# A graph network in one kernel: every engine keeps the emitted order, the timetable is told of three more buffers and gets new numbers

## The chip, the cores and the metric

The kernel runs on one core of one Trainium2 chip. The metric is the device time of one execution in microseconds (us); of several executions the median counts. Five engines matter here: TensorE (PE, matrix products, with weight loads shown as PEld), VectorE (DVE), ScalarE (ACT), GpSimd (POOL, hardly used) and SyncE (SP), which only issues transfers. Each has its own instruction queue, and the queues meet by semaphores.

## The reference

Sixteen graphs of 1024 nodes with 128 features each, a 0/1 adjacency with about 16 neighbours to a node, and four layers; each adds its output to `x` and normalises the rows.

```python
x = _layernorm(x + _L0_gnn_ref(x, adj, U))          # relu((mask^T x) U / deg)
x = _layernorm(x + _L1_gnn_ref(x, adj, Wv, ...))    # masked softmax attention, q, k, v with relu
x = _layernorm(x + _L2_gnn_ref(x, adj, W, a))       # GAT, 4 heads: leaky relu, softmax, sum
x = _layernorm(x + _L3_gnn_ref(x, adj, nodemask, ...))  # 3 x SAGE on a dilated adjacency, then linear
```

The last layer first dilates the adjacency. Row by row, a node with more than ten neighbours drops those whose running number is a multiple of half its count, and the column entry goes too:

```python
num = jnp.sum(nbi)
sf = jnp.where(num > T_DIL, (num + K_DIL - 1) // K_DIL, 1)
rank = jnp.cumsum(nbi)
rm = row & (rank % sf == 0)
carry = carry.at[n].set(row & keep)
carry = carry.at[:, n].set(carry[:, n] & keep)
```

## The kernel before

Two stages follow one another. `fuse` does layers 0 to 2 for 16 graphs (a batch below is one graph) and beside them the dilation. It leaves the features `x3` and the dilated adjacency `adt_d` in DRAM. `sage` does the last layer from there. This case changes only `fuse`.

A graph's adjacency is eight tiles of 128 rows by 1024. All work of `fuse` is written as ten generators, which run at the same time:

- `loads` and `signs`: adjacency tiles come in through SP, DVE makes the 0/1 pattern `has` (L332), ACT the complement `over` (L336).
- `dilate`: for the batch ahead. Eight scans on DVE (L354) give `ranked`, a running count along each row; PE turns blocks and DVE matches them (`turn`, `match`, L368, L378); two rounds and a last one decide what is dropped (ACT distances L426, DVE L441, PE counts L452); `lost` corrects (L495, ACT L519, DVE L528, which writes the dropped entries over `ranked`); `stays` makes the new pattern on PE (L541 to L547), and `store` evacuates it on ACT (L557) and sends it out through SP (L559).
- `layer0`: features (`py`) and the gather (L656).
- `layer1`, `scores`, `values`: keys, the attention scores (L744) with their minimum (L752) and exponential (L755), then transposes and the product with the values (L779).
- `layer2`, `sides`, `layer2_sums`: `weights` makes `st`, then the chain `top` (L882), `peak`, `peaks` (L887), `ps_cap` (L890), `cap` (L896), `ac` (L899), `src` (L917) and `pieces` (L924 to L933); `sides` makes sign tiles `sg` on ACT (L818) and masks them into `g` on DVE (L827); the sums use `pieces` against `has` (L968) and against `g` (L998).

Each generator yields a `Step` ahead of the instructions it is going to emit: an engine, a price in us, marks that must have been set, and places in rings of buffers that it takes or gives back. `Loom.run` is a planner in Python, run when the program is built. It keeps a clock for each engine. Of all heads it looks for the one that can start first, and among the steps of that engine which can start within a small window after it, it takes the one that is due first. Then the generator emits these instructions. A step's due time is the batch number times a period plus the phase of its part, with the prices of the steps before it in that part stretched by a factor:

```python
self.due = b * period + phase
self.due += self.step.cost * self.stretch
```

So the order in which the kernel emits is a whole timetable across engines. It knows the prices, a handoff time of 0.3 us between engines (0.5 us ahead of PE), and the rings it is told of: PSUM buffers (`two`, `one`, `dps`), `g`, `pr`, `a`, `w2k`, `over`. It didn't know that scans need `ranked` back, which has a single buffer (`p1`), that `sg` has two (`p2`), or that `adt` has two. The emitted order is then given to the compiler of the framework, which holds a dependency graph and a scheduler of its own: emitted order is a priority there, and each engine's queue can come out in another order.

All transfers named above are on SP's queue[...].

Of the kernel before, what the change touches and what calls it, by code (L numbers as in the profile page):

```python
# [7 lines left out]
F32 = mybir.dt.float32  # L8
# [6 lines left out]
F8 = mybir.dt.float8e4  # L15
# [5 lines left out]
P = 128  # L21
# [159 lines left out]
def fuse(S, ctx, a, x3, adt_d, viol, B=16):  # L181
# [20 lines left out]
    tc, nc = S.tc, S.nc  # L202
# [5 lines left out]
    N, TWOS, NEVER, ROUNDS, OVER = 8 * P, 2.0**24, 1e5, 2, 10  # L208
# [138 lines left out]
    def dilation(k, c):  # L347
# [2 lines left out]

        ranked[c] = p1.tile([P, 8, N], BF16, name="ranked")
        for r in range(8):
            yield Step("DVE", 2.2, after=(f"has {k} {r}",))
            V.tensor_tensor_scan(  # L354
                ranked[c][:, r, :], has[c][:, r, :], links[c][:, r, EDGE - 1 : EDGE - 1 + N].bitcast(U8),
                0.0, ALU.add, ALU.subtract,
            )
# [72 lines left out]
        for i in range(ROUNDS):  # L430
# [26 lines left out]
            sums = []  # L457
# [93 lines left out]

        def store(i, ps_n):
            r, f = i // 2, i % 2 * 512
            yield Step("ACT", 0.48, after=(f"stays {k} {i}",), give=[("dps", 0)])
            if f == 0:
                rows.append(p2.tile([P, N], F8, name="adt"))
            nc.scalar.activation(rows[-1][:, f : f + 512], ps_n, AF.Relu, scale=1.0 / LINK, saturate=False)  # L557
            if f:
                nc.sync.dma_start(adt_d[c, r], rows[-1])  # L559

        rows = []
# [4 lines left out]
    class Norm:  # L566


        def __init__(self, y):
            self.y = y  # L570
            self.st = sm.tile([P, 8, 6], F32, name="ln_st")

        def take(self, c):
            V.bn_stats(self.st[:, c, :], self.y[:, c, :])
# [1 line left out]
        def apply(self, mark):  # L576

            yield Step("DVE", 1.9)
            t = sm.tile([P, 6, 8, 1], F32, name="ln_t")
            both, apart, var, y, z, nb = (t[:, i, :, :] for i in range(6))  # L580
            e, o, se, so = (self.st[:, :, i : i + 1] for i in (1, 4, 2, 5))
            V.tensor_tensor(apart, e, o, ALU.subtract)
            V.tensor_tensor(var, se, so, ALU.add)
            V.scalar_tensor_tensor(apart, apart, P / 4.0, apart, ALU.mult, ALU.mult)
            V.tensor_tensor(var, var, apart, ALU.add)
            V.tensor_scalar(var, var, 1.0 / P, 1e-5, ALU.mult, ALU.add)

            V.tensor_scalar(y.bitcast(I32), var.bitcast(I32), -0.5, GUESS, ALU.mult, ALU.add)
            for _ in range(3):
                V.tensor_tensor(z, y, y, ALU.mult)  # L590
                V.scalar_tensor_tensor(z, z, -0.5, var, ALU.mult, ALU.mult)
                V.scalar_tensor_tensor(y, z, 1.5, y, ALU.add, ALU.mult)
            V.tensor_tensor(both, e, o, ALU.add)
            V.scalar_tensor_tensor(nb, both, -0.5, y, ALU.mult, ALU.mult)
            rs = y
            for q in range(2):
                yield Step("ACT", 1.55, mark=f"{mark} {q}")
                for c in range(4 * q, 4 * q + 4):
                    nc.scalar.activation(
                        self.y[:, c, :], self.y[:, c, :], AF.Identity, bias=nb[:, c, :], scale=rs[:, c, :]  # L600
                    )
# [156 lines left out]
    def values():  # L758
        for b in each:
            yield b, "values"  # L760
            yield Step(None, 0.0, after=(f"x1 {b} 1",))
            x2 = x01[b]
            norm = Norm(x2)
            for ib in range(8):
                yield Step("PE", 0.87, after=(f"pr {b} {ib}",), take=[("two", "p")], give=[("pr", ib)])
                pr, tot = made.pop((b, ib))
                ps_f = two.tile([P, 8, P], F32, name="ps_flip", tag="two")
                for q in range(2):
                    flip4(ps_f[:, 4 * q : 4 * q + 4, :], lambda c: pr[:, c * P : (c + 1) * P], q)
                yield Step("ACT", 0.89, give=[("two", "p")])  # L770
                pt = p2.tile([P, N], F32, name="pt")
                nc.scalar.copy(pt, ps_f.rearrange("p c d -> p (c d)"))  # L772
                vn = qkv[b][2]
                for q in range(2):
                    yield Step("PE", 0.89, after=(None, f"v {b}"), take=() if q else [("one", "a")])
                    if q == 0:
                        ps_a = one.tile([P, 512], F32, name="ps_a", tag="one")
                    for c in range(4 * q, 4 * q + 4):
                        nc.tensor.matmul(  # L779
                            ps_a[:, 0:P], pt[:, c * P : (c + 1) * P], vn[:, c, :], start=(c == 0), stop=(c == 7)  # L780
                        )
                yield Step("DVE", 0.6, give=[("one", "a")])
                rt = sm.tile([P, 1], F32, name="rt")
                V.reciprocal(rt, tot)
                V.scalar_tensor_tensor(
                    x2[:, ib, :], ps_a[:, 0:P], rt, x2[:, ib, :], ALU.mult, ALU.add
                )
                norm.take(ib)
            yield Step(None, 0.0, mark=f"early {b}")
            yield b, "norm 1"  # L790
            yield from norm.apply(f"x2 {b}")

            yield Step("DVE", 0.2)
            V.scalar_tensor_tensor(viol, lows[b], 1.0, viol, ALU.is_gt, ALU.max)
            V.scalar_tensor_tensor(viol, lows[b], -HI, viol, ALU.is_lt, ALU.max)
# [7 lines left out]
    def sides():  # L803

        for b in range(B):
            yield b, "sides"
            for h in range(H):
                for q in range(4):
                    for k in range(2):
                        yield Step(  # L810
                            "ACT", 1.04, after=(f"row {b} {h}", f"st {b}"),
                            take=[("g", (b, h, q // 2))] if k == 0 and q % 2 == 0 else (), mark=f"sg {b} {h} {q}",
                        )
                        st, side = stuff[b][0:2]
                        if k == 0:
                            sg = p2.tile([P, 2, N], I8, name="sg")
                        ib = 2 * q + k
                        nc.scalar.activation(  # L818
                            sg[:, k, :], rows[b, h], AF.Sign, bias=st[:, 1, h, ib : ib + 1], scale=-1.0
                        )  # L820
                    if q == 3 and h + 2 < H:
                        yield Step("SP", 0.2, lag=2.5, mark=f"row {b} {h + 2}")
                        row(b, h + 2)
                    yield Step("DVE", 0.6, after=(f"sg {b} {h} {q}",), mark=f"g {b} {h} {q // 2}" if q % 2 else None)
                    if q % 2 == 0:
                        side[h, q // 2] = p4.tile([P, 4, N], F8, name="g")
                    V.tensor_tensor(  # L827
                        side[h, q // 2][:, q % 2 * 2 : q % 2 * 2 + 2, :].bitcast(I16), sg.bitcast(I16),
                        has[b][:, 2 * q : 2 * q + 2, :].bitcast(I16), ALU.bitwise_and,
                    )  # L830
            yield Step(None, 0.0, mark=f"sides {b}")
# [116 lines left out]
    def layer2_sums():  # L948
        for b in each:
            yield b, "sums"  # L950
            yield from outputs(b)

    def outputs(b):
# [73 lines left out]
        for c in range(8):  # L1027
# [5 lines left out]

    batches = [*range(B), 0]
    loom = Loom(
        155.0, 0.1,
        {
            "loads": (364.0, 3.34),
            "signs": (813.0, 0.64),
            "ranks": (991.0, 0.88),  # L1040
            "match": (-250.0, 0.22),
            "round 0": (-892.0, 0.48),
            "round 1": (-332.0, 0.32),
            "last": (200.0, 0.95),
            "lost": (36.0, 0.46),
            "stays": (207.0, 1.52),
            "features": (480.0, 3.62),
            "gather": (327.0, 0.22),
            "norm 0": (-89.0, 0.53),
            "keys": (-51.0, 2.56),  # L1050
            "scores": (15.0, 0.20),
            "values": (198.0, 0.29),
            "norm 1": (530.0, 0.76),
            "sides": (467.0, 4.00),
            "weights": (294.0, 3.60),
            "pieces": (-104.0, 0.31),
            "sums": (303.0, 0.44),
            "weighted": (348.0, 0.59),
            "mean": (195.0, 0.44),
            "norm 2": (482.0, 0.20),  # L1060
        },
        two=2, one=2, dps=2, g=4, pr=2, a=2, w2k=4, over=OVER,
    )
    loom.run(
        layer2_sums(), sides(), values(), layer2(), scores(), layer1(), layer0(), signs(batches),
        loads(batches), dilate(batches),
    )


def sage(S, ctx, x3, mask, adt_d, viol, layers, Wl, bl, out, B=16):  # L1070
# [995 lines left out]
```

## Time and profile before

| what | value |
|---|---|
| median of three runs | 3487.2 us (3485.97 to 3496.11) |
| profiled execution | 3491.38 us, of which the span of the trace is 3489.7 us |
| mean granted PE clock over the span | 0.928 of full |
| fused stage, up to the last row of `adt` sent out | to about 2476 us of the span |
| last layer | from there to 3489.7 us |
| DVE scans L354 | 128 of 2272 ns, 286.8 us |
| ACT signs L818 | 512 of 1141 ns, 564.0 us |
| PE sums L998 / gather L656 / attention L779 | 392.9 / 433.7 / 272.7 us busy |
| transfers issued on SP | 520, at a mean of 63 GB/s |

A group of the profile is named by line, engine and tiles, "output<-input". "Idle before, releaser" is how long its engine stood still just ahead of it, and whose semaphore ended that. Busy time of PE counts an instruction that runs at half clock at its full length, so PE can be busy and slow. The granted clock is given for a stretch as a mean.

### The profile page before, as it was taken

The numbers are of one execution on the slowest core, as the hardware profiler recorded it, in microseconds if no ns is written. First come the engines' busy times: TensorE is split into PE (matmuls) and PEld (weight loads), VectorE is DVE, ScalarE is ACT, GpSimd is POOL, SyncE is SP. The second block draws the span as 40 slices with busy tenths as digits, with TensorE's granted clock in tenths as the row PEclk, the third lists the DMA queues.
The fourth block names the chain that finished last, engine by engine and source line by source line (L and its number), as shares of the span: only waits on it lengthen the run. The fifth ranks groups of instructions, "written<-read, shape, count | busy, mean of one in ns | idle before, by whom it ended". The sixth has DMA issues, their size and how long they took to land. (4 is left out here: it accounts for less than half of the span.)

```text
span 3489.7 us, 66022 instructions
## 1 busy us (share of the span) xinstructions
PE 3010.6 (86%) x25972; PEld 2377.9 (68%) x25972; DVE 2595.9 (74%) x7057; ACT 2323.7 (67%) x4149; POOL 2.0 (0%) x10
## 2 busy tenths in 40 slices
PE   4897988989898898988989889896599899989974
PEld 3676777777777777767777777775366666666653
DVE  4657687777868778687776868768388788888865
ACT  3786878878778787787878878777355444433334
POOL 0000000000000000000000000000000000000000
PEclk8898989989999999999989999998799999999987
DMA  4121112021120211202111120211333222212224
GB/s 109 37 67 37 61 44 92 25 80 51 48 86 25 80 56 50 77 22 92 49 56 57 42 92 25 74 42 39 76 101 91 73 61 61 61 49 61 61 88 122
DMA packets 224447, 219.97 MB, mean 63 GB/s; under 512 B 48000, under 2 KB 198528, under 8 KB 224128
## 3 DMA queue, kind: packets, MB, share of 16 engines
q1 hardware_dynamic: 224128, 215.67, 20.1%
q8 instruction: 205, 3.36, 0.4%
q14 instruction: 114, 0.93, 0.1%
HBM read 181.80 MB, written 33.82 MB: 62 GB/s over the span
## 5 line engine op out<-in xcount | busy, mean ns | idle before, releaser
L818 ACT ACTIVATE sg<-row,st 128x1024 int8<-128x1024 f32 x512 | 564.0, 1141 | 75.0 <-DVE g L827 55.7
L1165 PE MATMUL ps_g<-pz,ad 128*128 128x384 bf16 (+1 forms) x3072 | 535.8, 327 | 4.6 <-DMA ad<-adt_d 4.4
L1165 PEld LDWEIGHTS <-ad 128*128 128x128 fp8e4 x3072 | 297.6, 98 | 203.8 <-DMA ad<-adt_d 16.6
L998 PE MATMUL ps_b<-pieces,g 128*128 128x198 bf16 x4096 | 392.9, 249 | 3.8 <-DVE g L827 3.1
L998 PEld LDWEIGHTS <-g 128*128 128x128 fp8e4 x4096 | 354.6, 96 | 9.9 <-DVE g L827 4.6
L1182 ACT ACTIVATE sq<-xw 128x128 f32<-128x128 f32 x384 | 117.7, 307 | 305.7 <-DVE xw L1175 272.2
L779 PE MATMUL ps_a<-vn,pt 128*128 128x128 f32 x2048 | 272.7, 283 | 32.6 <-ACT pt L772 32.6
L426 ACT ACTIVATE x<-both,thr 128x1024 f16<-128x1024 bf16 (+7 forms) x384 | 276.1, 769 | 31.6 <-DVE thr L412 22.7
L744 PE MATMUL ps_s<-kt,qt 128*128 128x512 f32 x512 | 276.4, 622 | 24.0 <-ACT pr L755 14.5
L354 DVE TENSOR_TENSOR_SCAN ranked<-has 128x1024 bf16<-128x1024 fp8e4 x128 | 286.8, 2272 | 12.0 <-PE ps_n L547 11.9
L968 PE MATMUL ps_m<-pieces,has 128*128 128x132 bf16 x3072 | 224.7, 240 | 75.4 <-ACT pieces L930 45.0
L779 PEld LDWEIGHTS ps_a<-vn,pt 128*128 128x128 f32 x2048 | 248.6, 193 | 52.5 <-ACT pt L772 40.0
L968 PEld LDWEIGHTS <-has 128*128 128x128 fp8e4 x3072 | 217.7, 106 | 84.8 <-issue 84.4
L656 PE MATMUL ps_g<-py,has 128*128 128x128 bf16 (+1 forms) x3072 | 227.4, 241 | 35.8 <-DVE cap L896 30.6
L656 PEld LDWEIGHTS <-has 128*128 128x128 fp8e4 x3072 | 215.7, 109 | 37.5 <-issue 32.1
L557 ACT ACTIVATE adt<-ps_n 128x512 fp8e4<-128x512 f32 x256 | 146.5, 592 | 101.8 <-PE ps_n L547 92.8
L1174 DVE TENSOR_REDUCE t<-ps_g 128x128 f32<-128x384 f32 x384 | 206.2, 546 | 6.4 <-PE ps_g L1165 6.2
L1121 PE MATMUL ps_z<-wzx,raw 128*128 128x256 f32 x768 | 192.1, 393 | 10.7 <-ACT raw L1196 3.9
L752 DVE TENSOR_REDUCE low<-ps_s 128x1 f32<-128x1024 f32 x128 | 156.3, 1221 | 52.5 <-PE ps_s L748 48.5
L827 DVE TENSOR_TENSOR g<-sg,has 128x1024 int16<-128x1024 int16 x256 | 173.4, 679 | 28.4 <-ACT sg L818 27.5
L336 ACT ACTIVATE over<-a,under 128x1024 fp8e4<-128x1024 f32 x128 | 147.3, 1151 | 50.4 <-DMA a<-in_adj_dram 43.0
L1121 PEld LDWEIGHTS ps_z<-wzx,raw 128*128 128x128 f32 x768 | 144.1, 195 | 45.9 <-PE ps_y L1142 13.6
(255 smaller groups left out, 5928.8 us busy)
## 6 DMA issues: line engine op xcount, KB each, us to landing
a<-in_adj_dram SPq DMA_DIRECT2D x136, 512.0 KB, 3.7
ad<-adt_d SPq DMA_DIRECT2D x384, 128.0 KB, 2.3
row<-t_d SPq DMA_DIRECT2D x64, 512.0 KB, 3.8
adt_d<-adt SPq DMA_DIRECT2D x128, 128.0 KB, 1.7
xn<-x SPq DMA_DIRECT2D x32, 512.0 KB, 4.2
x<-in_x_dram SPq DMA_DIRECT2D x16, 512.0 KB, 5.4
x<-x SPq DMA_DIRECT2D x16, 512.0 KB, 4.2
out_dram<-y SPq DMA_DIRECT2D x16, 512.0 KB, 3.2
```

The lines of the kernel that those rows point to most:

```text
L354: V.tensor_tensor_scan(ranked[c][:, r, :], has[c][:, r, :], links[c][:, r, EDGE - 1 : EDGE - 1 + N].bitcast(U8), 0.0, ALU.add, ALU.subtract,)
L426: nc.scalar.activation(x, both[:, at[r] : at[r + 1]], AF.Abs, bias=far[:, r : r + 1], scale=2.0)
L656: nc.tensor.matmul(ps_g[:, k, 0:e], has[b][:, jb, ib * P : (ib + 1) * P], py[:, jb, q * P : q * P + e], start=(jb == 0 and q == 2), stop=( ...
L744: nc.tensor.matmul(ps_s[:, f : f + 512], qt[:, ib * P : (ib + 1) * P], kt[:, f : f + 512], start=True, stop=False,)
L779: nc.tensor.matmul(ps_a[:, 0:P], pt[:, c * P : (c + 1) * P], vn[:, c, :], start=(c == 0), stop=(c == 7))
L818: nc.scalar.activation(sg[:, k, :], rows[b, h], AF.Sign, bias=st[:, 1, h, ib : ib + 1], scale=-1.0)
L827: V.tensor_tensor(side[h, q // 2][:, q % 2 * 2 : q % 2 * 2 + 2, :].bitcast(I16), sg.bitcast(I16), has[b][:, 2 * q : 2 * q + 2, :].bitcast( ...
L968: nc.tensor.matmul(ps_m[:, u // 2, o : o + H * D1], has[b][:, ib, jb * P : (jb + 1) * P], pieces[:, ib, 1, :, t, :], start=(t == 0 and ib ...
L998: nc.tensor.matmul(ps_b[:, u // 2, (u % 2) * 2 * W3 : (u % 2 + 1) * 2 * W3], side[h, q][:, k, jb * P : (jb + 1) * P], pieces[:, 4 * q + k, ...
L1121: nc.tensor.matmul(ps_z[:, k, :], raw[:, b, c * P : (c + 1) * P], wzx, start=True, stop=True)
L1165: nc.tensor.matmul(ps_g[:, 0:width], adt[jb][:, ib * P : (ib + 1) * P], pz[:, jb, 0:width], start=(jb == 0), stop=(jb == 7),)
L1174: nc.vector.tensor_reduce(t, ps_g[:, 0 : 3 * P].rearrange("p (t d) -> p d t", t=3), AX.X, ALU.add)
```

## The change

The whole of it is in `fuse`. All calls of the planner's generators are put under a region in which every engine issues in the order of emission:

```diff
-    loom.run(
-        layer2_sums(), sides(), values(), layer2(), scores(), layer1(), layer0(), signs(batches),
-        loads(batches), dilate(batches),
-    )
+    with tc.manual_schedule():
+        loom.run(
+            layer2_sums(), sides(), values(), layer2(), scores(), layer1(), layer0(), signs(batches),
+            loads(batches), dilate(batches),
+        )
```

The planner gets a mark that scans wait for, a ring for `sg`, and a ring for `adt`, whose tile has three buffers now; the store is a step on SP:

```diff
-            yield Step("DVE", 2.2, after=(f"has {k} {r}",))
+            yield Step("DVE", 2.2, after=(f"has {k} {r}",) + ((f"stays {k - 1} {14 + r // 4}",) if k > 1 else ()))
...
-            yield Step("ACT", 0.48, after=(f"stays {k} {i}",), give=[("dps", 0)])
+            yield Step(
+                "ACT", 0.48, after=(f"stays {k} {i}",), give=[("dps", 0)], take=[] if f else [("adt", r)]
+            )
             if f == 0:
-                rows.append(p2.tile([P, N], F8, name="adt"))
+                rows.append(p2.tile([P, N], F8, name="adt", bufs=3))
...
             if f:
+                yield Step("SP", 0.2, lag=2.0, give=[("adt", r)])
                 nc.sync.dma_start(adt_d[c, r], rows[-1])
...
-                            take=[("g", (b, h, q // 2))] if k == 0 and q % 2 == 0 else (), mark=f"sg {b} {h} {q}",
+                            take=([("sg", 0)] if k == 0 else [])
+                            + ([("g", (b, h, q // 2))] if k == 0 and q % 2 == 0 else []),
+                            mark=f"sg {b} {h} {q}",
...
-                    yield Step("DVE", 0.6, after=(f"sg {b} {h} {q}",), mark=f"g {b} {h} {q // 2}" if q % 2 else None)
+                    yield Step(
+                        "DVE", 0.6, after=(f"sg {b} {h} {q}",), mark=f"g {b} {h} {q // 2}" if q % 2 else None,
+                        give=[("sg", 0)],
+                    )
```

Two small tiles of the row norms get four buffers instead of three:

```diff
-            self.st = sm.tile([P, 8, 6], F32, name="ln_st")
+            self.st = sm.tile([P, 8, 6], F32, name="ln_st", bufs=4)
...
-            t = sm.tile([P, 6, 8, 1], F32, name="ln_t")
+            t = sm.tile([P, 6, 8, 1], F32, name="ln_t", bufs=4)
```

And the timetable has new numbers (period and window, then phase and stretch of each part), all 23 parts; those that the text speaks of:

```diff
-        155.0, 0.1,
+        120.0, 0.2,
...
-            "signs": (813.0, 0.64),
-            "ranks": (991.0, 0.88),
+            "signs": (689.0, 0.90),
+            "ranks": (1332.0, 0.88),
...
-            "gather": (327.0, 0.22),
+            "gather": (255.0, 4.00),
...
-            "weights": (294.0, 3.60),
-            "pieces": (-104.0, 0.31),
-            "sums": (303.0, 0.44),
+            "weights": (131.0, 3.60),
+            "pieces": (-107.0, 0.20),
+            "sums": (122.0, 0.28),
...
-        two=2, one=2, dps=2, g=4, pr=2, a=2, w2k=4, over=OVER,
+        two=2, one=2, dps=2, g=4, pr=2, a=2, w2k=4, sg=2, adt=3, over=OVER,
```

No instruction that computes is added or taken away.

More of the change, by code (lines that the diff above doesn't have):

```diff
@@ L1035, in fuse @@
     loom = Loom(
-        155.0, 0.1,
+        120.0, 0.2,
         {
-            "loads": (364.0, 3.34),
-            "signs": (813.0, 0.64),
-            "ranks": (991.0, 0.88),
[L1041 to L1047, printed above, removed]
-            "gather": (327.0, 0.22),
[L1049 to L1054, printed above, removed]
-            "weights": (294.0, 3.60),
-            "pieces": (-104.0, 0.31),
-            "sums": (303.0, 0.44),
-            "weighted": (348.0, 0.59),
-            "mean": (195.0, 0.44),
-            "norm 2": (482.0, 0.20),
+            "loads": (694.0, 3.07),
+            "signs": (689.0, 0.90),
+            "ranks": (1332.0, 0.88),
+            "match": (-325.0, 0.67),
+            "round 0": (-901.0, 1.38),
+            "round 1": (-618.0, 0.50),
+            "last": (193.0, 1.56),
+            "lost": (159.0, 1.86),
+            "stays": (212.0, 4.00),
+            "features": (362.0, 0.22),
+            "gather": (255.0, 4.00),
+            "norm 0": (-188.0, 4.00),
+            "keys": (-172.0, 3.20),
+            "scores": (139.0, 2.59),
+            "values": (231.0, 0.25),
+            "norm 1": (753.0, 0.92),
+            "sides": (547.0, 4.00),
+            "weights": (131.0, 3.60),
+            "pieces": (-107.0, 0.20),
+            "sums": (122.0, 0.28),
+            "weighted": (348.0, 0.42),
+            "mean": (40.0, 2.17),
+            "norm 2": (884.0, 0.74),
```

## The prediction

> **What bounds the kernel now.** First the page, engine shares: no engine is full over the whole run, TensorE (PE) is nearest.
>
> ```profile
> PE 3010.6 (86%) x25972; PEld 2377.9 (68%) x25972; DVE 2595.9 (74%) x7057; ACT 2323.7 (67%) x4149; POOL 2.0 (0%) x10
> ```
>
> The chain that ended last has five pieces, all ACT outputs of the last 5 us, so it says nothing of the stage that is edited. That stage (the fused layers 0 to 2 with the dilation) ends at 2476 us of the span: the last adjacency rows leave there and the first load of the last layer is issued. I looked for its period: the scans (L354) begin at 1039, 1186, 1332, 1479, 1626 us, so a batch takes 147 us. Then I cut a period in two by the view of stages (columns: length, busy us and count of PE, weight loads, DVE, ACT, POOL, then PE clock and DMA):
>
> ```profile
> 1186.00:1216.00 30.00, 18.22 (x200) 17.57 (x200) 29.98 (x48) 22.82 (x29) 0.00 (x0) 0.72 0.24 79
> 1332.00:1363.00 31.00, 19.30 (x214) 18.64 (x213) 30.55 (x50) 22.81 (x29) 0.00 (x0) 0.72 0.27 87
> ...
> 1216.00:1332.00 116.00, 110.57 (x1091) 90.52 (x1089) 82.34 (x254) 96.24 (x154) 0.00 (x0) 1.00 0.15 51
> 1363.00:1479.00 116.00, 110.02 (x1085) 90.11 (x1083) 81.76 (x253) 96.12 (x154) 0.00 (x0) 1.00 0.16 52
> ```
>
> For 116 us PE is 95% busy at full clock. For the other 30, where the eight scans run, DVE is full, PE idles 11.8 us and has 0.72 of its clock. All that an order can win per batch lies there. The waits of that stretch (us, times, longest) name it:
>
> ```profile
> PE ps_cap L890 <- DVE peaks L887: 5.0, 1, 5.0
> PE ps_m L968 <- ACT pieces L930: 3.3, 1, 3.3
> ...
> PE ps_g L656 <- DVE cap L896: 2.3, 1, 2.3
> ```
>
> With 0.9 and 0.3 us more before ps_m they make the 11.8. Over the run, PE's wait at ps_cap is 69.9 us in 15 times, one a batch. The timeline shows why, on DVE
>
> ```profile
> 1186.02 8.84 DVE L354 TENSOR_TENSOR_SCAN ranked<-has 128x1024 bf16<-128x1024 fp8e4 x4 [0.45 <-PE ps_n L547]
> 1194.77 0.25 DVE L885 TENSOR_REDUCE peak<-ps_top 8x1 f32<-8x128 f32 x1
> ...
> 1195.55 0.21 DVE L887 TENSOR_SCALAR peaks<-ident,peak 8x8 f32<-8x8 f32 x1
> ...
> 1196.36 2.27 DVE L354 TENSOR_TENSOR_SCAN ranked<-has 128x1024 bf16<-128x1024 fp8e4 x1
> 1198.56 0.13 DVE L896 COPY cap<-ps_cap 128x8 f32<-128x8 f32 x1
> 1198.61 2.27 DVE L354 TENSOR_TENSOR_SCAN ranked<-has 128x1024 bf16<-128x1024 fp8e4 x1
> 1200.81 0.15 DVE L899 TENSOR_TENSOR ac<-st,cap 128x32 f32<-128x32 f32 x1
> ```
>
> and on PE (start, us, then the instruction and the idle time before it):
>
> ```profile
> 1189.47 0.27 PE L882 MATMUL ps_top<-ident,top 128*8 128x128 f32 x1
> ...
> 1195.82 0.59 PE L890 MATMUL ps_cap<-peaks,ones 8*128 8x8 f32 x2 [4.95 <-DVE peaks L887]
> 1198.74 5.31 PE L656 MATMUL ps_g<-py,has 128*128 128x129 bf16 x48 [2.33 <-DVE cap L896]
> ```
>
> A short chain, top, peak, peaks, cap, ac, src, pieces, must pass DVE several times before the sums of layer 2 may start. Six scans of 2.2 us stand in its way, four of them in a row. PE meanwhile stands at ps_cap, with 5.31 us of gather matmuls behind it. Someone ordered PE as if DVE came free sooner than it does. It wasn't the kernel: a memset of `gone` (L417), emitted after the scans and matches of batch 1, runs 2.00 us into the span. Before the change the compiler reorders what the timetable emits.
>
> [...] 0.25 us of peak stands behind 8.84 us of scans, 48 gather matmuls behind two tiny ones. [...] Here 30 us at 0.72 are 2 x 0.28 x 30 = 16.8 us at half clock; the records place them at 1193.8 to 1204.0 and 1207.4 to 1214.3, and PE is busy for 5.85 + 4.99 = 10.8 us of them, so 5.4 us are lost. [...] the scan waited for stays 11.9 us in the whole run (14 times).
>
> **The change, part by part.** Per period PE is busy 18.2 + 110.6 = 128.8 of 146.5 us; less the 5.4 it needs 123.4 at full clock.
>
> 1. *Every engine keeps the emitted order.* No instruction comes or goes. The timetable prices a scan at 2.2 us, and four in a row took 8.84, so 2.21 each: its price is right. It picks among the steps that could start within a window of the first (0.1 us before, 0.2 now) the one that is due first. Scans were due at b x 155 + 991, now at b x 120 + 1332; beside the next batch's scans stand weights (294, now 131) and pieces (-104, now -107). So scans come last, by more than before, and run only where nothing else could start: at most one can get ahead of the chain at each of its returns to DVE. Returns with a handoff from another engine are three: peak (with peaks), cap, ac. Three scans, 3 x 2.21 = 6.6 us, stay in the way instead of six (13.3), so 6.6 us of PE's 11.8 go. Bounds: nothing (three scans that moved delay something equal) to all 11.8 (gather put ahead of ps_cap, 5.31 us of it is ready).
>
> 2. *Clock.* The lost 5.4 us come down with the idle time, but [...] 5 us of idle stay. I take a third, 1.8; bounds 0 and 5.4.
>
> 3. *Scans wait in the plan for stays 14 and 15 of the batch before.* The buffer `ranked` is single, so the wait was there already. Its own idle is at most 11.9 us in all. [...] under a kept order a timetable that didn't know it would stop DVE each batch. I take 0; bounds -12 and +15 (1 us a batch).
>
> 4. *sg has a ring of two.* ACT idled 55.7 us in 24 times for DVE's g, with adt, x and pr behind it. ACT is busy 119 of 147 us a batch, so this is off the path: 0; bounds -15 (a quarter of it) and 0.
>
> 5. *A third store buffer, and the store as a step of SP's own.* PE waited 7.5 us for adt's evacuation, ACT 3.7 us for its store. The 128 stores are as many as before, at other places of SP's queue, where SP already waited 411.3 us for adt (126 times, longest 19.6). [...] ACT's sg waited 10.4 us for rows, DVE's has 51.7 us for adjacency. Other work hides this: I take 0; bounds -11 and +50 (were both waits to double).
>
> 6. *Fourth buffers for two small norm tiles:* no instruction, no visible wait: 0. *Phases and stretches:* their effect is in 1; what they do to the fill (weighted sums start at 205 us) and the tail (they end at 2439) I can't derive: 0, bounds -30 and +30. The last layer, from 2476 us on, has the same code.
>
> Sum: 6.6 + 1.8 = 8.4 us a batch; ps_cap waits in 15, so 126 us. The profiled execution took 3491.4 us (span 3489.7), 4.2 above the median 3487.2; 3491.4 - 126 = 3365, and with the same 4.2 off 3361 as the median.
>
> **The rivals.** A is the forecast, 3361, own range 3300 to 3430 (4 to 12 us a batch). Between A and the rivals lies how far the bubble is filled.
>
> B, the bubble goes whole: the 30 us get as dense as the 116. Then a period is 123.4 / 0.953 = 129.5, 17 us less, 255 in all: 3232. For it: ready gather stood behind ps_cap. Against: DVE is full in that stretch, so the scans only move.
>
> C, the loop of the dilation is the real bound: scan, match, two rounds, lost, stays, then the next scan, on one `ranked` buffer. For it: stays end at 1185 and 1332 where scans begin at 1186 and 1332. Against: DVE waited there only 11.9 us. The fill of PE then gains little, 2 us a batch: 3457. That the kept order changes nothing (the compiler had kept most of it) would end at 3487; the early memset speaks against it.
>
> D, slower: that same loop gets longer, because scans are due last and DVE may no longer slip them in. Each us by which the eighth scan ends later is a us of every period. Spread over 42 us instead of 30, with the 8.4 saved, a period is 3.6 longer, 15 x 3.6 = 54: 3541. It decides from 8.4 us of delay on, four scans' length. For it: 95 us of other DVE work a batch, all due earlier. Against: DVE is 82 of 116 busy after the scans, so they needn't wait long.
>
> **How the numbers follow.** A 0.42, B 0.18, C 0.15, no change 0.05, D 0.20. A measurement of this kernel tells 0.3% (10 us) from no change; A, B and C are faster, so 0.75 faster, 0.05 same, 0.20 slower. The range goes from just below B, 3225, to 3510, where it takes in C, no change and D's mild end; about 0.07 lies below, 0.13 above.
>
> **What would show it.** Right: a period of some 138 us between scans of successive batches; PE's wait at ps_cap for peaks far under 69.9 us; no four scans in a row ahead of peak; clock over 0.93 in the fused stage; the last layer 1013 us long as now. B would show 130 us and hardly any half clock. D would show scans spread over more than 38 us, with PE's bubble moved to the matches. Wrong altogether: a new wait of PE, ACT's row or DVE's adjacency loads, that comes once a batch and is 8 us or more.

## The result, and the profile after

The changed kernel takes 3519.8 us (median of five runs, 3516.0 to 3527.7); the kernel before took 3486.0 beside it. The ratio is 1.0099, with a 95% interval of 1.0078 to 1.0119: about 34 us slower, where 126 us less was forecast. The profiled execution took 3525.4 us, its span is 3523.7.

The fused stage gives nearly all of it. Its last store is issued at 2503.5 us of the span (2471.6 before); from there to the end it is 1020 us, where it was 1018. Of these 32 us, 22 come in the eight middle batches and 9 after them. First the engine shares on the page of the changed kernel:

```profile
PE 3027.2 (86%) x25972; PEld 2383.6 (68%) x25972; DVE 2665.7 (76%) x7057; ACT 2326.8 (66%) x4149; POOL 2.0 (0%) x10
```

The counts are those of before; DVE is busy 70 us longer with the same 7057 instructions (why, wasn't followed up). The scans begin at 1040, 1202, 1341, 1503, 1641 us, so the period now alternates between 162 and 139 us. Over the eight batches up to 2242 us it is 150.1 us; before, over the same eight (1039 to 2219), 147.4. Two periods of the changed kernel by stages (length, then busy us and count of PE, weight loads, DVE, ACT, POOL, then PE clock and DMA):

```profile
1010.00:1040.00 30.00, 28.05 (x286) 23.91 (x284) 21.82 (x76) 23.62 (x44) 0.00 (x0) 0.94 0.42 132
1040.00:1093.00 53.00, 43.64 (x537) 40.49 (x534) 44.16 (x84) 41.42 (x64) 0.00 (x0) 0.90 0.28 86
1093.00:1143.00 50.00, 45.42 (x391) 35.63 (x388) 41.15 (x116) 39.47 (x51) 0.00 (x0) 0.97 0.01 1
1143.00:1201.00 58.00, 51.46 (x525) 42.69 (x525) 34.11 (x112) 46.31 (x89) 0.00 (x0) 0.97 0.31 101
1201.00:1241.00 40.00, 28.94 (x224) 21.61 (x224) 38.52 (x66) 27.61 (x39) 0.00 (x0) 0.79 0.18 54
1241.00:1311.00 70.00, 66.03 (x651) 54.97 (x649) 54.70 (x153) 61.06 (x85) 0.00 (x0) 1.00 0.02 9
sum 301.00, PE 263.55 PEld 219.30 DVE 234.46 ACT 239.49 POOL 0.00; mean PE 43.92 PEld 36.55 DVE 39.08 ACT 39.92 POOL 0.00
```

The second and the fifth line are the stretches of the scans: 53 and 40 us long, where they took 30 and 31. In one of them PE is now 82% busy, in the other 72%. PE idles 37.5 of these 301 us, 18.7 a batch; the period of before had 17.7 (146.5 less 128.8). So the hole was spread, not filled. PE's waits over the whole run (us, times, longest) say where it went. In the kernel before:

```profile
PE ps_cap L890 <- DVE peaks L887: 69.9, 15, 6.9
...
PE ps_s L452 <- DVE part L441: 7.7, 20, 0.6
PE ps_t L368 <- DVE both L378: 7.5, 4, 3.7
PE ps_n L541 <- ACT adt L557: 7.5, 22, 1.2
```

and in the changed kernel:

```profile
PE ps_s L452 <- DVE part L441: 34.6, 30, 7.1
...
PE ps_t L368 <- DVE both L378: 25.0, 26, 5.6
...
PE ps_n L541 <- ACT adt L559: 22.2, 19, 1.9
...
PE ps_top L890 <- DVE top L887: 17.3, 7, 3.2
PE ps_cap L898 <- ACT x L602: 16.5, 4, 4.1
...
PE ps_cap L898 <- DVE peaks L895: 15.8, 7, 4.1
```

`ps_cap` is down from 69.9 us to 32.3, and 17.3 us of waiting for `top`, one step earlier in the same chain, are new. In their place stand the rounds of the dilation (L452), the turned blocks (L368) and the evacuation of the stays (L541): 81.8 us against 22.7. These are instructions of the loop that makes the dilated adjacency.

The scans still stand in the way of the chain. In one of the two batches, on DVE of the changed kernel (start, us, instruction):

```profile
1202.00 4.45 DVE L354 TENSOR_TENSOR_SCAN ranked<-has 128x1024 bf16<-128x1024 fp8e4 x2
...
1206.44 2.26 DVE L354 TENSOR_TENSOR_SCAN ranked<-has 128x1024 bf16<-128x1024 fp8e4 x1
1208.63 0.18 DVE L887 TENSOR_REDUCE top<-st 128x8 f32<-128x64 f32 x1
...
1212.69 0.27 DVE L893 TENSOR_REDUCE peak<-ps_top 8x1 f32<-8x128 f32 x1
...
1214.45 2.29 DVE L354 TENSOR_TENSOR_SCAN ranked<-has 128x1024 bf16<-128x1024 fp8e4 x1
1216.65 0.14 DVE L904 COPY cap<-ps_cap 128x8 f32<-128x8 f32 x1
...
1216.94 2.29 DVE L354 TENSOR_TENSOR_SCAN ranked<-has 128x1024 bf16<-128x1024 fp8e4 x1
1219.14 0.67 DVE L925 TENSOR_TENSOR src<-wh,ac 128x512 f32<-128x512 f32 x1
```

Three scans pass ahead of `top`, one ahead of `cap` and one ahead of `src`: five, not three. `peak` stands 3.5 us behind the small instructions of a row norm (L577 to L597) that were emitted ahead of it. The stays of the batch before end at 1199 us, the buffer `ranked` is free, and eight scans come into reach at once.

### The profile page after: what moved, and what is told of

Its sections match the earlier page's. It is cut to its first block, busy times and chain, and to the rows that moved or that the text cites. A ratio compares the mean times of both kernels' runs of the same rounds, so it can differ in the third digit from the quotient of the medians.

```text
span 3523.7 us, 66295 instructions
## 1 busy us (share of the span) xinstructions
PE 3027.2 (86%) x25972; PEld 2383.6 (68%) x25972; DVE 2665.7 (76%) x7057; ACT 2326.8 (66%) x4149; POOL 2.0 (0%) x10
## 5 line engine op out<-in xcount | busy, mean ns | idle before, releaser
L823 ACT ACTIVATE sg<-row,st 128x1024 int8<-128x1024 f32 x512 | 567.6, 1146 | 37.2 <-DMA row<-t_d 32.1
L1006 PE MATMUL ps_b<-pieces,g 128*128 128x198 bf16 x4096 | 402.2, 249 | 6.1 <-DVE g L835 3.3
L1006 PEld LDWEIGHTS <-g 128*128 128x128 fp8e4 x4096 | 352.4, 96 | 22.7 <-issue 12.5
L782 PE MATMUL ps_a<-vn,pt 128*128 128x128 f32 x2048 | 273.6, 283 | 12.1 <-ACT pt L775 11.9
L976 PEld LDWEIGHTS <-has 128*128 128x128 fp8e4 x3072 | 210.5, 104 | 51.9 <-issue 51.8
L659 PE MATMUL ps_g<-py,has 128*128 128x128 bf16 (+1 forms) x3072 | 218.7, 237 | 27.0 <-DVE cap L904 11.2
L659 PEld LDWEIGHTS <-has 128*128 128x128 fp8e4 x3072 | 208.7, 107 | 29.2 <-issue 23.8
L835 DVE TENSOR_TENSOR g<-sg,has 128x1024 int16<-128x1024 int16 x256 | 174.0, 684 | 66.8 <-ACT sg L823 65.9
L1130 PE MATMUL ps_z<-wzx,raw 128*128 128x256 f32 x768 | 192.5, 394 | 11.9 <-DVE xw L1138 5.1
L602 ACT ACTIVATE x<-x,ln_t 128x128 f32<-128x128 f32 x384 | 154.8, 483 | 47.5 <-DVE ln_t L597 47.5
```

What stands on the lines that cost most here:

```text
L659: nc.tensor.matmul(ps_g[:, k, 0:e], has[b][:, jb, ib * P : (ib + 1) * P], py[:, jb, q * P : q * P + e], start=(jb == 0 and q == 2), stop=( ...
L782: nc.tensor.matmul(ps_a[:, 0:P], pt[:, c * P : (c + 1) * P], vn[:, c, :], start=(c == 0), stop=(c == 7))
L823: nc.scalar.activation(sg[:, k, :], rows[b, h], AF.Sign, bias=st[:, 1, h, ib : ib + 1], scale=-1.0)
L835: V.tensor_tensor(side[h, q // 2][:, q % 2 * 2 : q % 2 * 2 + 2, :].bitcast(I16), sg.bitcast(I16), has[b][:, 2 * q : 2 * q + 2, :].bitcast( ...
L976: nc.tensor.matmul(ps_m[:, u // 2, o : o + H * D1], has[b][:, ib, jb * P : (jb + 1) * P], pieces[:, ib, 1, :, t, :], start=(t == 0 and ib ...
L1006: nc.tensor.matmul(ps_b[:, u // 2, (u % 2) * 2 * W3 : (u % 2 + 1) * 2 * W3], side[h, q][:, k, jb * P : (jb + 1) * P], pieces[:, 4 * q + k, ...
```

## The experiments

All times are medians; each ratio is to the kernel before, run beside it on the same chip, with its 95% interval in brackets. `period` is the mean distance between first scans, over the eight batches of the middle.

### Order and timetable taken apart

The order alone, on the kernel before (**e3_before_kept**):

```diff
-    loom.run(
+    with tc.manual_schedule():
+        loom.run(
```

> The kernel before with nothing but the region that keeps the order. Theory 'the kept order costs because the plan doesn't know of the buffers': DVE stops at the first scan of each batch until the stays of the batch before are over (the wait ranked L354 for ps_n over 100 us in all) and the time is 3560 us or more. Theory 'order kept is right by itself': 3400 us or less.

3568.7 us, ratio 1.0239 [1.0220, 1.0258], period 152.7. The order of that timetable, kept, is worse than what the compiler makes of it. Two of DVE's waits in this run have grown most; the second, of the scans, is its largest on PE:

```profile
DVE lone L979 <- ACT every L973: 141.0, 15, 10.0
DVE ranked L354 <- PE ps_n L547: 59.9, 14, 5.2
```

Before, the scans' wait came to 11.9 us; over 100 were expected. Now DVE stands idle ahead of the waiting scan for 4.3 us a batch (59.9 us in 14 times). It isn't the only stop that grew: the reduction `lone` of layer 2 waits for ACT even longer, 141.0 us against 41.2 before, so the 83 us can't all be put down to the scans.

The changed kernel with the old numbers of the timetable (**e1_kept_oldtable**), and the changed kernel without the kept order (**e2_free_newtable**):

```diff
-        120.0, 0.2,
+        155.0, 0.1,
...
-            "ranks": (1332.0, 0.88),
+            "ranks": (991.0, 0.88),
...
```

```diff
-    with tc.manual_schedule():
-        loom.run(
+    loom.run(
```

> The changed kernel with the period, window, phases and stretches of before put back; order kept, the three buffers known to the planner. Theory 'the kept order costs, the new numbers repaid part of it': slower than the changed kernel, 3570 to 3650 us. Theory 'the new numbers are the harm, the kept order is harmless': faster than the changed kernel, 3380 to 3480 us, with fewer scans in a row ahead of peak.

> The changed kernel without the region that keeps the order: new numbers, rings and buffers stay, the compiler reorders again. Theory 'the kept order costs': back near the kernel before, 3450 to 3500 us. Theory 'the new numbers are the harm': 3510 us or more, as the changed kernel.

3697.2 us, 1.0607 [1.0586, 1.0627], period 163.8; and 3507.4 us, 1.0065 [1.0040, 1.0090], period 150.3. The first is slower than even its theory had it; the second lies between the two theories: 21 of the 34 us are there while the compiler still reorders (new numbers, rings and buffers), and keeping the order adds 12. With the new numbers and the compiler free the batches alternate too (156 and 144 us), with the old numbers and the order kept they don't (164 each), so the alternation comes with the numbers.

The changed kernel with its order and numbers, but without what the planner was told of scans, `sg` and `adt` (**e8_kept_unknowing**):

```diff
-            yield Step("DVE", 2.2, after=(f"has {k} {r}",) + ((f"stays {k - 1} {14 + r // 4}",) if k > 1 else ()))
+            yield Step("DVE", 2.2, after=(f"has {k} {r}",))
...
-                yield Step("SP", 0.2, lag=2.0, give=[("adt", r)])
```

> The changed kernel, order kept and new numbers, but the planner isn't told of the scans' wait, of sg's two buffers, or of the store (no step on SP, no ring for adt; the tile keeps three buffers). Theory 'the numbers are fitted to what the planner knows': 3560 to 3640 us. Theory 'the knowledge is worth little': within 15 us of the changed kernel.

3561.3 us, 1.0209 [1.0192, 1.0226], period 153.7. Together, with the order kept (us):

| planner | old numbers | new numbers |
|---|---|---|
| isn't told | 3568.7 | 3561.3 |
| is told | 3697.2 | 3519.8 |

Order alone costs 83 us. New numbers alone then give 7, telling the planner alone costs 128, both together give 49: they only fit as a pair, and the pair doesn't pay for the order. (The second row has the added buffers too, and so has the new column.) With the compiler free to reorder, the kernels with the two timetables lie 21 us apart (3486.0 untold, 3507.4 told); kept, 177 (3519.8 and 3697.2, both told).

Could the fault be DVE's order alone? The kernel before with the order kept on all engines but DVE (**e7_before_kept_but_dve**):

```diff
-    loom.run(
+    with tc.manual_schedule(engines={mybir.EngineType.PE, mybir.EngineType.Activation, mybir.EngineType.SP, mybir.EngineType.Pool}):
+        loom.run(
```

> The kernel before with the order kept on PE, ACT, SP and POOL, and DVE left to the compiler. Theory 'what the compiler repaired was DVE standing at scans': most of the 83 us that keeping all four orders cost come back, 3480 to 3510 us. Theory 'it is PE's order or the queues as a whole': 3540 us or more.

3600.0 us, 1.0320 [1.0303, 1.0337]: worse than all orders kept (3568.7). Setting DVE free does not cure it, as the second theory had it; here the orders that come from two schedulers fit each other less than either whole.

### Are scans that are due last the fault?

The cheapest test of the slower rival is to make them due early (**e5_scans_early**):

```diff
-            "ranks": (1332.0, 0.88),
+            "ranks": (300.0, 0.88),
```

> The changed kernel with one number of the timetable other: the phase of the scans is 300 instead of 1332, so that scans are due early and run close together. Theory 'the loop scan to stays to scan is too long because scans are due last': the scans of a batch end within 25 us of their first, and the time falls to 3440 to 3490 us. Theory 'scans in a row starve PE, the loop isn't what sets the period': PE's waits for DVE grow and the time is 3600 us or more.

3677.4 us, 1.0539 [1.0522, 1.0557], period 162.8. The scans do shrink to 20 us, but the stays now take 53 us (30 and 23 in the changed kernel), and the period grows: the time that the second theory gave. PE's largest wait in this run is

```profile
PE ps_t L368 <- DVE both L378: 221.1, 80, 11.6
```

PE turns blocks that DVE, full of scans, can't match: in the 20 us from 1250 on it is busy for 19.86. One phase can't be moved by itself. Whether the loop sets the period this run doesn't tell; the last runs below do.

### A timetable searched for the kept order

Same program, same planner, other numbers, searched on the planner's own clock (**e4_kept_searched**; its table without the kept order, **e6_searched_free**; a longer search, **e9_searched_longer**):

```diff
-        120.0, 0.2,
+        120.0, 0.4,
...
-            "ranks": (1332.0, 0.88),
+            "ranks": (10615.0, 0.93),
...
```

> The changed kernel with another set of period, window, phases and stretches, picked because the planner's own clock ends some 40 us earlier with it. Theory 'with the order kept the time follows the planner's timetable': 40 us or so below the changed kernel, 3460 to 3490 us. Theory 'stalls on the chip that the planner doesn't see decide': within 15 us of the changed kernel, or above.

> The timetable of e4_kept_searched, but the compiler may reorder. Theory 'a timetable acts through the kept order': its 60 us over the changed kernel's table are gone, 3490 to 3540 us. Theory 'the table is better whoever orders': 3470 us or less.

> As e4_kept_searched, with a timetable found by a longer search on the planner's own clock (10 us or so earlier by it). Theory 'with the order kept the time follows the timetable': 3440 to 3455 us. Theory 'what is left is stalls the planner doesn't see': 3460 us as e4_kept_searched, or more.

3460.2 us, 0.9928 [0.9909, 0.9947]; free, 3500.9 us, 1.0038 [1.0024, 1.0052]; longer, 3443.0 us, 0.9872 [0.9848, 0.9895]. With a table that fits, a kept order beats the compiler's by 41 us at the same numbers, where the table of the change loses 12 (3519.8 and 3507.4). But the periods are 147.6 and 145.2, hardly below 147.4: the gain of the first lies in the fill, where the eight batches begin at 1004 us instead of 1039. And the wait that the forecast was about is gone in it:

```profile
PE ps_cap L898 <- DVE peaks L895: 3.2, 13, 0.2
```

With 3.2 us of it left where 69.9 were, the period is what it was. So this wait was not what set it.

### The loop through one buffer

In most of these runs the next scan starts within 2 us of the end of the stays of the batch before (3.4 in every second batch of the changed kernel, 3.8 with the old numbers told, 5 to 9 with early scans, up to 12 untold). To test this loop the scans first got a planner part of their own, still waiting for the stays, with a table searched (**e10_scans_apart**); then the stays were made to read `has` instead of `ranked`, and the scans to wait for the last dropped entries only (**e11_loop_open**, with its own search). This run leaves out the dropping of edges from the stored adjacency: the matrices keep their shapes, but what is stored is not dilated.

```diff
-                    "DVE", 2.2, after=(f"has {k} {r}",) + ((f"stays {k - 1} 15",) if k > 1 else ()),
+                    "DVE", 2.2, after=(f"has {k} {r}",) + ((f"drop {k - 1} 7",) if k > 1 else ()),
...
-            nc.tensor.matmul(ps_n, less, drop[:, r, f : f + 512], start=True, stop=False)
+            nc.tensor.matmul(ps_n, less, has[c][:, r, f : f + 512], start=True, stop=False)
```

> The scans made a generator of their own in the planner, so that they are planned apart from the rest of the dilation (matches wait for the mark of their scan, turns for the adjacency rows they read); same work, same buffers, order kept, a timetable searched for this. Theory 'time follows the timetable': 3425 to 3445 us. Theory 'unseen stalls': 3460 us or more.

> As e10_scans_apart, but stays reads the pattern has where it read ranked: the adjacency that is stored is then not the dilated one (that part of the computation is left out), with as many matmuls of the same shapes. So the scans of the next batch may start after lost instead of after stays. Theory 'the loop scan to stays to scan on the single ranked buffer sets the period': 40 us or more below e10_scans_apart. Theory 'it isn't the loop, the queues are full of waits on each other': within 25 us of it.

3448.5 us, 0.9886 [0.9863, 0.9909], period 145.9, between its two theories: a planner part of their own gives the scans nothing (3443.0 without). With the loop open 3367.5 us, 0.9654 [0.9627, 0.9681], period 140.1. The matmuls of the stays last as long as before (means of 380 and 220 ns, 379 and 219 with the scans apart), so it isn't their other operand.

The same without leaving anything out (**e12_own_tile**): the dropped entries go to a tile of their own, one byte an element. Room comes from one buffer for `xt` and `xt2`, single `sums`, two `adt`, and nine tiles of `over` instead of ten; table searched.

```diff
-        drop = ranked[c]
+        drop = p1.tile([P, 8, N], F8, name="drop")
...
-                    drop[:, r, :], apart.pop(r), 2.0 * CODE, mark[:, r : r + 1], ALU.min, ALU.is_equal
+                    drop[:, r, :], apart.pop(r), 2.0 * CODE, mark[:, r : r + 1], ALU.min, ALU.is_equal,
+                    saturate=False,
```

> The loop of the one buffer of ranked entries, opened without leaving anything out: the dropped entries are written to a tile of their own, so that the next batch's scans wait for the last dropped entries (the step after the stays' input is complete) and not for the stays themselves; the order is kept, the timetable searched for this form; room is made by narrower rings elsewhere. Theory (the single buffer's loop, scans to dropped entries to stays to scans, sets the period once the order is kept): 3360 to 3395 us, within some 25 us of the run in which the stays read other data, 40 us or more below the run with the scans apart, and a period near 141 us. Rival (that run gained because its stays waited for nothing real, or the narrower rings and the further tile cost what the loop gives): 3430 us or more, period 145 us or longer.

3376.1 us, 0.9668 [0.9651, 0.9685], period 141.4, in the theory's range and faster than both kernels.

Its table was searched anew and its rings are narrower, so two more runs keep its instructions and buffers and close the loop in the plan alone, with the same table (**e13_own_tile_wait**) and with one searched as long (**e14_own_tile_wait_searched**):

```diff
-                    "DVE", 2.2, after=(f"has {k} {r}",) + ((f"drop {k - 1} 7",) if k > 1 else ()),
+                    "DVE", 2.2, after=(f"has {k} {r}",) + ((f"stays {k - 1} 15",) if k > 1 else ()),
```

> The kernel with the dropped entries in a tile of their own, unchanged but for one word of the planner: scans wait in the plan for the stays of the batch before, as in the changed kernel, although no buffer asks for it any more. Same instructions, same buffers, same timetable; only the order can differ. If the loop through the stays sets the period: 3430 us or more (55 us, 3.5 us a period, or more above the run without that wait), the first scan again at the end of the stays. If the table or the smaller rings gave the gain: within 25 us of 3376.

> As the run before it, with the timetable searched again for this wait, as long as it was searched for the form without it, so that the closed loop has its best chance. Loop: 3420 to 3480 us, 45 us or more above the open loop, with the next scan at the end of the stays in every batch. Rival (the gain was the table's fit and not the loop): within 25 us of 3376.

3786.7 us, 1.0866 [1.0848, 1.0885], and 3449.5 us, 0.9899 [0.9882, 0.9916]. The first shows again how little a table is worth for a planner that knows other waits. The second settles it with the run before it: 73 us (3449.5 less 3376.1) for one wait in the plan, each with a table searched for it, and the time of the run with the scans apart (3448.5). The tables differ within this pair, so all searched runs count: with the loop closed they took 3460.2, 3443.0, 3448.5 and 3449.5 us, with the loop open 3367.5 and 3376.1. The two traces, stays and scans of one batch each (durations min/median/max in ns, then first and last start in us), with the loop closed:

```profile
L552 PE MATMUL ps_n<-less,drop x64: 217/219/314, 1114.4 to 1144.6; 128*128 128x128 bf16 x64
```

```profile
L357 DVE TENSOR_TENSOR_SCAN ranked<-has x8: 2269/2272/2282, 1144.3 to 1174.1; 128x1024 bf16<-128x1024 fp8e4 x8
```

and with the loop open:

```profile
L552 PE MATMUL ps_n<-less,drop x64: 217/219/220, 1093.5 to 1128.2; 128*128 128x128 bf16 x64
```

```profile
L357 DVE TENSOR_TENSOR_SCAN ranked<-has x8: 2268/2275/2286, 1091.4 to 1129.2; 128x1024 bf16<-128x1024 fp8e4 x8
```

Closed, the scans follow the stays; open, they run beside them, though still spread over 40 us. The period is 5.1 us shorter (146.5 and 141.4), which over 15 batches makes 77 us, where 73 were measured. Two periods of the open loop by stages (scans, the rest, scans, the rest):

```profile
1091.00:1131.00 40.00, 36.02 (x410) 31.84 (x408) 38.37 (x87) 27.47 (x55) 0.00 (x0) 0.96 0.45 145
1131.00:1232.00 101.00, 92.52 (x889) 76.42 (x891) 79.49 (x216) 90.97 (x129) 0.00 (x0) 0.97 0.09 28
1232.00:1272.00 40.00, 34.58 (x409) 30.22 (x407) 38.02 (x87) 27.56 (x55) 0.00 (x0) 1.00 0.44 145
1272.00:1374.00 102.00, 91.68 (x886) 75.13 (x888) 79.63 (x215) 90.61 (x128) 0.00 (x0) 0.97 0.09 27
```

The stretch of the scans holds 410 matmuls in 40 us at the clock of the rest (0.96 and 1.00), where the kernel before had 200 in 30 us at 0.72: the stays give PE work while DVE scans. What the forecast wanted from a better order came only with one tile more. That tile with the compiler free to reorder was not run.

## Why the prediction was wrong

**The bound.** "All that an order can win per batch lies there", in the 30 us of the scans, was read from PE alone. With the order kept, the bound is the loop on the single `ranked` buffer (3443 to 3460 us closed, 3368 and 3376 open). That it also bound the kernel before, whose order the compiler makes, is likely but not shown: there the loop was never opened. The prediction had this loop as rivals C and D and set it aside because DVE waited there only 11.9 us. That is no argument: in the changed kernel the scans have next to no idle time before them (0.2 us in all), since DVE does other work until the buffer comes free, and the loop is as closed. The starts and ends of the stages that the rival named (stays end 1185, next scan 1186) were the better evidence. Opening the loop was worth 73 us (3449.5 and 3376.1).

**Step 1**, the order, 6.6 us a batch: this is the term that failed. It took what PE would no longer wait at the chain for time won. "At most one can get ahead of the chain at each of its returns" didn't hold (five passed in the batch shown). Even so PE's waits at `ps_cap`, at `ps_m` and at `ps_g` for `cap` fell from 175.6 to 89.3 us, 86 less where 15 times 6.6 makes 99 (63 less with those at `ps_top`). But another 59 us appeared in the loop's own waits (L452, L368, L541), and over the whole fused stage PE stood idle 369 us, where it had been 358. Order and new numbers without what the planner is told, which is the step as the prediction cut it (with the added buffers), came to 73 us more than the kernel before beside it (3561.3 and 3488.7).

The step also counted the scans' move as free. Later scans lengthen their part of the loop from 31 to 46.5 us (the mean of 53 and 40). From the last scan to the first of the stays it shrank from 94 to 76 us, the stays took 26 instead of 22, in every second batch the next scan begins 3.4 us after them, and the net is 2.7 us longer. The prediction's own D, with a spread of 42 us and a period 3.6 us longer (3541), came nearest, 21 us too slow. Its direction and its signs were right, its rule that each us of later scans is a us of every period was not: scans that end 15 us later cost 2.7, and in the longer search they spread over 45 us with a period of 145.2. So part of its nearness is luck.

**Step 2**, the clock, 1.8: nothing. The low clock of the kernel before is there (0.50 and 0.51 in the two windows that the prediction names); that a third of the 5.4 us would come back was the author's estimate. The granted clock is 0.94 in the eight middle batches before and after. In the stretches of the scans it is 0.90 and 0.79, where PE idles 18% and 28% of the time; before it was 0.72, with 38 to 39% idle. Whether the idle time lowers it wasn't tried.

**Step 3**, the scans' wait in the plan, 0: its sign depends on the table, -41 us with the new numbers (3561.3 to 3519.8, together with the other two rings, which weren't tried alone) and +128 with the old. The bounds of -12 and +15 were taken from DVE's idle time, which is not where this wait acts.

**Steps 4 and 5**: ACT's wait for `g` fell from 55.7 to 5.0 us, but DVE's for `sg` rose from 27.5 to 65.9, and ACT's wait for rows rose from 10.4 to 32.1. SP's wait at the stores for `adt` came out the same (411.3 and 411.4 us) and DVE's for adjacency fell from 51.7 to 32.3. No cost of these appears apart from step 3's; they weren't separated. (Two entries in the table of before are off: SP issues 872 transfers, not 520, and the gather keeps PE busy 227.4 us; 433.7 adds up two shapes that run interleaved.)

**Step 6**, phases and stretches, 0 with bounds of 30: under a kept order they are the largest term. The runs that differ in the numbers alone span 254 us (3443.0 with the longer search, 3519.8, 3697.2 with the old numbers), against 7 us with the compiler free (3507.4 and 3500.9).

**What should have shown it**: of the signs named for the forecast, three came: the wait at `ps_cap` fell, the last layer stayed, and in 12 of 15 batches three scans stand ahead of `peak`, not four. They came without the time, so they were no signs of it. Period and clock did not come. D's signs did: scans over more than 38 us, and PE's gaps moved to the matches and rounds. The alternation of 162 and 139 us was expected by neither; what in the new numbers makes the two kinds of batch differ wasn't tried.

## What to carry to other kernels

Before pricing an order, look for a loop from batch to batch through one buffer: list when each holder ends and the next begins, and distrust a small wait there: the scans of the changed kernel waited 0.2 us in all, with the loop closed, because DVE was busy with other work. Idle time taken from one wait is not yet time won: here 86 us of PE's waits at the chain went and the kernel got 34 us slower. A kept order is worth only what its timetable is worth: the same switch cost 83 us with the old table and 12 with the new one, and gave 41 with one searched for it. Where the loop is the bound, a tile that lets the next holder start earlier can be worth more than the order: here it beat every order tried within the loop (3376.1 us, 3443.0 the best of them).

## What the runs showed of the hardware

The comparison that writes the dropped entries took longer into one-byte elements (with `saturate=False`, which wasn't tried alone) than into bf16, with the same input; here the changed kernel and then the one with the tile of its own (min/median/max ns):

```profile
L528 DVE TENSOR_SCALAR ranked<-x,thr x128: 468/486/491, 159.5 to 2481.2; 128x1024 bf16<-128x1024 f16 x128
```

```profile
L532 DVE TENSOR_SCALAR drop<-x,thr x128: 736/746/754, 189.1 to 2333.1; 128x1024 fp8e4<-128x1024 f16 x128
```

That is 260 ns each, 33 us of DVE's time over the run, and little of it can have reached the time: 3376.1 us with it, 3367.5 in the other run with the loop open, which writes bf16 (its table and its rings are others too). On PE the one-byte operand made no difference in the same two runs: the median matmul took 379 ns where the tile streams through (L541, then L546) and 219 ns where it is loaded as weights (L547, then L552), in both.
